# Two layers of graph network on one Trainium2 core: the state's halves are turned by transposing transfers instead of 32x32 blocks and a trip through DRAM

## The chip, the core and the metric

The kernel runs on one core of a Trainium2 chip. Its engines are TensorE (PE, matrix products), VectorE (DVE), ScalarE (ACT), GpSimd (POOL) and SyncE (SP), which here only issues transfers. The metric is the device time of one execution in microseconds (us), as the median of several runs; lower is better.

## The reference

The input x holds 32 independent sequences of 512 nodes with 128 features, and adj is one 512x512 matrix of zeros and ones that all share. Layer 0 is attention over the graph, layer 1 five steps of a gated recurrence. Each starts from a layer norm with a ReLU, and each is added to x:

```
h = relu(layernorm(x));  x = x + leaky(softmax(mask(adj) + leaky(e_src + e_dst)) @ (h W) + b)
h = relu(layernorm(x))
repeat 5 times:
    m  = adj @ h                       # the same for "in" and "out"
    z  = sigmoid([m, m] w3^T + b3 + h u3^T + bu3)
    r  = sigmoid([m, m] w4^T + b4 + h u3^T + bu3)
    hv = tanh([m, m] w5^T + b5 + (r*h) u5^T + bu5)
    h  = (1 - z) h + z hv
x = x + h
```

## The kernel before

The state of a sequence in layer 1 is kept twice. `hT` (128 features on the partitions, 512 nodes along them, float32) feeds the gates and is updated in place. The product with adj needs the other layout, nodes on the partitions, and it needs it as two float16 halves, `hi` (h rounded) and `lo` (what the rounding left), so that eight float16 matmuls with `adjT` give m (L1032). After each step `hT` must therefore be turned and split again before the next step of this sequence can begin.

A step of `recurrence(b, step, ...)` runs so: eight matmuls for m, a copy of it by ScalarE (`mT`, L1043), two products for the r gate (`g`, L1051 and L1052) and its tanh (L1057), r times h by VectorE (`rh`, L1064), the z gate (L1072) and its tanh (L1084), two products for the candidate (`v`, L1095 and L1096) and its tanh (`hv`, L1102), and three VectorE instructions for the new `hT` (L1109, L1115, L1118). Sigmoids are made of tanh, with the weights scaled for it.

`hT` is turned in one of two ways. The direct way is four 128x128 transposes by TensorE into PSUM (`h`, L1156), from where the halves are cast and subtracted. The other way is a VectorE transpose of 32x32 blocks (`blocks`, L1170), one store to DRAM (`way`, L1176), four loads that put the blocks into place (`rows`, L1181), and then the same cast by ScalarE (`hi`, L1009) and subtraction by VectorE (`lo`, L1007). Which way a turn goes is decided by this line, with SHORT = 3 and SHORT_END = 4:

```
nth = 5 * b + WIDTH * step
if nth < 5 * SHORT or (step >= STEPS - 2 and b >= B - SHORT_END):
```

WIDTH is 6, so the direct way is taken for six turns of the first sequences, and for the last two steps of the last four. After the fifth step the turned h goes to the output: for 28 sequences through blocks and DRAM too, then scaled and added to x1.

Layer 0 of a sequence (norm, turn, products hp and av, attention weights) is woven between the steps of others. About six sequences are under way at once, in ten slots of state. Each piece of work is a Task with an engine, an estimated length, a key (its due time), the tasks that it needs and the buffers that it takes. `plan` simulates the engines with the estimates of COST and the landing times (LANDING = 5000 ns for a transfer) and fixes the order of every engine's instructions at build time; on the chip each engine goes through its own list in this order and waits where a needed result is late. SP's list holds the loads of x, the transfers of the turns and the stores of results; POOL's holds the transfers of layer 0's turns.

Of the kernel before, what the change touches and what calls it, by code (L numbers as in the profile page):

```python
# [10 lines left out]
F32 = mybir.dt.float32  # L11
F16 = mybir.dt.float16
AF = mybir.ActivationFunctionType
ALU = mybir.AluOpType

P = 128
# [10 lines left out]
WIDTH = 6  # L27
SLOTS = 10
DIRECT = 4
SHORT = 3  # L30
ENDING = 1
SHORT_END = 4
EARLY = 6
# [13 lines left out]
}  # L47
FIRST_IDLE, IDLE = 32, 36
LANDING = 5000
BRANCH = 150  # L50

WAIT = {"DVE": 200, "ACT": 200}
BANKS = {"m": 2, "g": 3, "v": 2, "o": 4, "bank": 8}
BUFFERS = {
    "x": 4, "h0": 2, "h0T": 2, "hw": 3, "pt0": 2, "pt1": 2, "pt2": 2, "pt3": 2, "o_": 2, "hN": 2,
    "es": 2, "lines": 2, "blocks": 2, "rows": 3, "res": 2, "mT": 4, "r": 2, "rh": 3, "z": 3,
    "hv": 2, "d": 2, "way": 4, "turn": 4, "line": 4,
}


# [224 lines left out]
def gat_then_gated_gnn_kernel(  # L285
# [20 lines left out]
    nc = tc.nc  # L306
    B, N, D = x.shape
# [10 lines left out]
    pools = {  # L318
        n: fast.enter_context(tc.tile_pool(name=f"w{n}", bufs=n)) for n in set(BUFFERS.values())
    }  # L320
    dram = fast.enter_context(tc.tile_pool(name="dram", bufs=4, space=bass.MemoryType.DRAM))
    psum = fast.enter_context(tc.tile_pool(name="psum", bufs=8, space=bass.MemoryType.PSUM))
    pin = tc.keep_in_program_order
    tasks = []

    def add(*args, **kwargs):
        tasks.append(Task(*args, **kwargs))
        return tasks[-1]

    def new(buffer, name, shape=(P, N)):  # L330
        tag = buffer.tags[0]
        if "bank" in buffer.tags:
            buffer.tile = psum.tile([P, N], F32, tag="bank", name=name)
        elif tag in ("way", "turn", "line"):
            buffer.tile = dram.tile(list(shape), F32, tag=tag, name=name)
        else:
            buffer.tile = pools[BUFFERS[tag]].tile(list(shape), F32, tag=tag, name=name)
        return buffer.tile


# [30 lines left out]
    hTs = [state.tile([P, N], F32, name=f"hT_{s}") for s in range(SLOTS)]  # L371

    his = [state.tile([P, K, D], F16, name=f"hi_{s}") for s in range(SLOTS)]
    los = [state.tile([P, K, D], F16, name=f"lo_{s}") for s in range(SLOTS)]
# [15 lines left out]
    def load_x(b, key=None, lands=3000):  # L390
        f = Buffer("x")

        def issue():
            pin(nc.sync.dma_start(out=new(f, f"x_{b}", (P, K, D)), in_=x_r[b]))

        needs = () if key else (bias_loaded,)
        load = add("SP", [1], key or 5 * (b - LEAD) * STEP, issue, needs, (f,), lands=lands)
        return f, load
# [35 lines left out]
    def idle():  # L434
        pin(nc.tensor.transpose((f_idle.tile or new(f_idle, "idle"))[:, :P], ident, ident))  # L435
# [14 lines left out]
    def issue():  # L450
        pin(nc.tensor.matmul(
            new(f_as, "as_ps")[:, : 2 * D], lhsT=ones[0:1, :],
            rhs=avecs.rearrange("o i d -> o (i d)"), start=True, stop=True,
        ))
# [263 lines left out]
    def blockwise(dst, src, which, keys, needs, buffers, by_halves):  # L718
# [11 lines left out]
        def store(g):  # L730
            def issue():
                if way.tile is None:
                    new(way, f"turn_{which}", (K * P, P))
                pin(nc.gpsimd.dma_start(  # L734
                    out=way.tile.rearrange("(e r) (g q) -> g r e q", r=Q, g=G)[g],
                    in_=f.tile[ts(g, Q)].rearrange("r (e q) -> r e q", q=Q),
                ))

            return issue

        stores = []
        for g in range(G):
            stores.append(add("POOL", [1], keys(1), store(g), (t,), (f, way),
                              lands=LANDING))

# [5 lines left out]

        return add("POOL", [1], keys(2), load, stores, (*buffers, way), lands=LANDING + 1500)

# [10 lines left out]
    def layer0(b):  # L764
# [7 lines left out]
        def keys(i):  # L772
            return begin + length * (base[0] + i) / parts
# [77 lines left out]
        else:  # L851
# [11 lines left out]
            def store(k):  # L863
                def issue():
                    if way.tile is None:
                        new(way, f"line_{b}", (K, P))
                    pin(nc.gpsimd.dma_start(
                        out=way.tile[k].rearrange("(g q) -> g q", g=G),
                        in_=f_lines.tile[k * rep :: Q],
                    ))  # L870

                return issue

            stores = []
            for k in range(K):
                stores.append(add("POOL", [1], keys(1), store(k), (t,),
                                  (f_lines, way), lands=LANDING))

# [5 lines left out]

            t = add("POOL", [1], keys(2), spread, stores, (way, f_es), lands=LANDING + 1500)
        base[0] = 15
# [126 lines left out]
    def recurrence(b, step, halved, turned):  # L1013
# [5 lines left out]
        def keys(i):  # L1019
            return key + i * STEP / 4  # L1020

        hT = hTs[b % SLOTS]
# [16 lines left out]
        high, low = halved  # L1039
# [29 lines left out]
        last = step == STEPS - 1  # L1069
# [66 lines left out]
        if near:  # L1136
            t_keep = add("DVE", [512], keys(3.5) - STEP, keep, (t_z,), (f_z, f_d))
            t = add("DVE", [512], keys(5), gated_hv, (t, t_z), (f_z, f_hv))
            turned = add("DVE", [512], keys(5), twice, (t, t_keep), (f_hv, f_d))
            to_turn = f_d  # L1140
        else:
            t = add("DVE", [512], keys(5), differ, (t,), (f_hv, f_d))
            t = add("DVE", [512], keys(5), gated, (t, t_z), (f_z, f_d))
            turned = add("DVE", [512], keys(5), update, (t,), (f_d,))
            to_turn = None

        nth = 5 * b + WIDTH * step
        if nth < 5 * SHORT or (step >= STEPS - 2 and b >= B - SHORT_END):

            f = Buffer("o", "bank")  # L1150

            def turn():
                h_ps = new(f, f"h_{b}_{step}")
                h = to_turn.tile if to_turn else hT
                for k in range(K):
                    pin(nc.tensor.transpose(h_ps[:, ts(k, P)], h[:, ts(k, P)], ident))  # L1156

            needs = (add("PE", [256] * K, keys(6), turn, (turned,),
                         (f, to_turn) if to_turn else (f,)),)
            view = ("p k d -> p k d", {})  # L1160

            def src():
                return f.tile.rearrange("p (k d) -> p k d", k=K)
        else:


            f_b, way, f = Buffer("blocks"), Buffer("way"), Buffer("rows")

            def blocks():
                pin(nc.vector.transpose(  # L1170
                    new(f_b, f"blocks_{b}_{step}").rearrange("p (g k q) -> p g k q", g=G, k=K),
                    hT.rearrange("p (k g q) -> p g k q", g=G, k=K),
                ))

            def store():
                pin(nc.sync.dma_start(out=new(way, f"way_{b}_{step}"), in_=f_b.tile))  # L1176

            def load(g):
                def issue():
                    rows = f.tile or new(f, f"rows_{b}_{step}", (P, G, N // G))  # L1180
                    pin(nc.sync.dma_start(  # L1181
                        out=rows[ts(g, Q)],
                        in_=way.tile.rearrange("(a q) (g e) -> g q a e", a=G, g=G)[g],
                    ))

                return issue

            t = add("DVE", [512], keys(6), blocks, (turned,), (f_b,))
            t = add("SP", [1], keys(6), store, (t,), (f_b, way), lands=LANDING)
            needs = []  # L1190
            for g in range(G):
                needs.append(add("SP", [1], keys(6), load(g), (t,), (way, f),
                                 lands=LANDING))
            view = ("p k (a q) -> p a k q", {"a": G})

            def src():
                return f.tile.rearrange("p a (k q) -> p a k q", k=K)

        if not last:
            return halves(b, src, keys(8), needs, (f,), view[0], **view[1]), turned  # L1200
        f_res = Buffer("res")

        def lower():
            res = new(f_res, f"res_{b}", (P, K, D))
            pin(nc.scalar.mul(res.rearrange(view[0], **view[1]), src(), 1 / LIFT))
# [4 lines left out]
        def result_at_once():  # L1210
            pin(nc.vector.scalar_tensor_tensor(
                new(f_res, f"res_{b}", (P, K, D)), src(), (0.5 if near else 1) / LIFT,
                x1s[b % SLOTS], ALU.mult, ALU.add,
            ))
# [4 lines left out]
        else:  # L1219
            finished[b] = add("DVE", [512], keys(8), result_at_once, needs, (f, f_res))  # L1220
        add("SP", [1], keys(8), lambda: pin(nc.sync.dma_start(out=out_r[b], in_=f_res.tile)),
            (finished[b],), (f_res,), lands=LANDING)

    def ending(b, keys, t_rh, t_z, buffers):

# [82 lines left out]
    for b in range(B):  # L1308
        halved, turned = layer0(b)
        for step in range(STEPS):  # L1310
            made = recurrence(b, step, halved, turned)
            if made:
                halved, turned = made
    order = plan(tasks)
    for t in order[:-BRANCH]:
        t.issue()

    general = nc.values_load(flag[0:1, 0:1])
    for t in order[-BRANCH:]:
        t.issue()  # L1320
# [44 lines left out]
```

## Time and profile before

| | before |
|---|---|
| median of 3 runs | 1141.48 us (1141.41 to 1142.08) |
| span of the profiled execution, first to last instruction | 1139.7 us |
| what the median has beside that span | 1.8 us |
| TensorE busy | 1133.1 us, 99% |
| VectorE busy | 946.9 us, 83% |
| ScalarE busy | 659.3 us, 58% |
| GpSimd busy | 350.7 us, 31% |
| moved by transfers | 132.88 MB, mean 117 GB/s |

The profile is of one execution. Its page gives the busy time of each engine, the busy share in 40 slices of the span, the chain of work that ended last, followed back from the last instruction, and the costliest groups of instructions: line, engine, operation, tiles, shapes and count, then the busy time in us and the mean of one in ns, then the idle time of the engine just before them and what ended it. For transfers it gives the time from issue to landing. Of which of the runs the profile was taken is not told; the 1.8 us are the difference between their median and its span. The timeline lists instructions in order of time. A matmul's record runs on while the next one has begun, so the records overlap.

### The profile page before, as it was taken

To read this page: it belongs to the slowest core of one execution; us is meant where nothing else is said; L and a number is where in the kernel's file an instruction comes from. 1 tells how busy PE (TensorE), PEld (TensorE's weight loads), DVE (VectorE), ACT (ScalarE), POOL (GpSimd) and SP (SyncE) were. 2 spreads that over 40 slices of the span, in tenths; PEclk is the share of its full clock that TensorE was granted. 3 is DMA by queue.
4 is the path that set the end of the run, shared out by engine and by line. 5 is a ranking of instruction groups with operands and counts; after the bars stand their busy time and mean duration, and the time that the engine had idled before them with its cause. 6 is when DMAs were issued, how large, how long until landed. Compare 5 with 4: busy or idle time off the path is not lost.

```text
span 1139.7 us, 15186 instructions
## 1 busy us (share of the span) xinstructions
PE 1133.1 (99%) x4373; PEld 599.0 (53%) x4373; DVE 946.9 (83%) x2124; ACT 659.3 (58%) x1297; POOL 350.7 (31%) x503
## 2 busy tenths in 40 slices
PE   9999999999999999999999999999999999999998
PEld 8665554555455545555554555546555555444444
DVE  7888988889789888987898878989898998765764
ACT  6755566555755665564656645575656655554553
POOL 4345324132424234341443315243455321100000
PEclk9999999999999999999999999999999999999999
DMA  3114435353445444443444435444445433332311
GB/s 107 45 49 118 131 106 145 109 142 114 139 115 151 121 139 130 125 125 111 141 138 138 122 110 146 144 132 129 131 128 154 129 103 103 103 98 76 112 37 66
DMA packets 133915, 132.88 MB, mean 117 GB/s; under 512 B 22082, under 2 KB 97988, under 8 KB 133700
## 3 DMA queue, kind: packets, MB, share of 16 engines
q1 hardware_dynamic: 116066, 94.89, 26.6%
q0 software_dynamic: 17472, 36.79, 13.1%
q8 instruction: 36, 0.59, 0.2%
q14 instruction: 51, 0.42, 0.1%
q10 hardware_dynamic: 290, 0.20, 0.1%
HBM read 70.39 MB, written 61.40 MB: 116 GB/s over the span
## 4 chain that ended last, share of the span: by engine, by line
PE 99%; ACT 0%; DVE 0%; issue 0%; POOL 0%; POOLq 0%; DVEq 0%
PE m L1032 24%; PE g L1072 12%; PE g L1051 12%; PE g L1052 12%; PE v L1096 12%; PE v L1095 12%; PE av L923 10%; PE hp L807 3%; PE idle L435 1%; PE h L1156 0%; PE t_a L702 0%; PE t_b L702 0%; PE v_end L1256 0%; PE es L842 0%; PE end L1274 0%; PE at_ps L489 0%
## 5 line engine op out<-in xcount | busy, mean ns | idle before, releaser
L1057 ACT ACTIVATE rs<-g,zrb 128x512 f32<-128x512 f32 x160 | 109.8, 686 | 142.0 <-PE g L1052 138.7
L1102 ACT ACTIVATE hv<-v,vb 128x512 f32<-128x512 f32 x159 | 109.0, 686 | 124.1 <-PE v L1096 123.8
L1051 PE MATMUL g<-hT,u3T 128*128 128x512 f32 x320 | 163.5, 592 | 0.0
L1052 PE MATMUL g<-mT,w4sT 128*128 128x512 f32 x320 | 163.4, 592 | 0.0
L1072 PE MATMUL g<-mT,w3dT 128*128 128x512 f32 x320 | 163.2, 594 | 0.0
L1032 PE MATMUL m<-adjT,hi 128*128 128x512 f16 x640 | 162.4, 379 | 0.0
L1095 PE MATMUL v<-mT,w5sT 128*128 128x512 f32 x318 | 162.4, 592 | 0.0
L1096 PE MATMUL v<-rh,u5hT 128*128 128x512 f32 x318 | 162.4, 592 | 0.0
L1032 PE MATMUL m<-adjT,lo 128*128 128x512 f16 x640 | 161.5, 379 | 0.0
L1043 ACT COPY mT<-m 128x512 f32<-128x512 f32 x160 | 93.6, 585 | 113.6 <-PE m L1032 112.8
L1064 DVE SCALAR_TENSOR_TENSOR rh<-rs,hT 128x512 f32<-128x512 f32 x160 | 108.5, 682 | 54.3 <-ACT rs L1057 53.8
L1109 DVE SCALAR_TENSOR_TENSOR d<-hv,hT 128x512 f32<-128x512 f32 x158 | 107.5, 681 | 54.4 <-ACT hv L1102 53.9
L1084 ACT ACTIVATE zs<-g,zrb 128x512 f32<-128x512 f32 x160 | 109.7, 685 | 64.0 <-PE g L1072 63.1
L923 PEld LDWEIGHTS av<-hw,pt 128*128 128x128 f32 x1024 | 122.2, 191 | 16.6 <-issue 12.7
L923 PE MATMUL av<-hw,pt 128*128 128x129 f32 x1024 | 123.8, 275 | 0.2 <-ACT adjT L498 0.2
L1118 DVE SCALAR_TENSOR_TENSOR hT<-d,hT 128x512 f32<-128x512 f32 x158 | 109.2, 691 | 11.8 <-PE m L1032 0.5
L1032 PEld LDWEIGHTS <-hi 128*128 128x128 f16 x640 | 62.6, 98 | 102.2 <-issue 49.5
L1115 DVE SCALAR_TENSOR_TENSOR d<-zs,d 128x512 f32<-128x512 f32 x158 | 109.1, 691 | 4.8
L1032 PEld LDWEIGHTS <-lo 128*128 128x128 f16 x640 | 62.7, 98 | 88.1 <-issue 22.7
L645 POOL TENSOR_TENSOR rs_b<-ve_b,mhalf 128x4 f32<-128x4 f32 x32 | 36.2, 1132 | 228.2 <-DVE ve_b L625 195.2
L1170 DVE STREAM_TRANSPOSE blocks<-hT 128x512 f32<-128x512 f32 x146 | 102.8, 706 | 4.1 <-DMA way<-blocks 1.4
L734 POOL DMA_DIRECT2D turn_b<-blocks_b x112 | 73.8, 664 | 91.0 <-DVE blocks_b L724 89.3
(140 smaller groups left out, 1434.0 us busy)
## 6 DMA issues: line engine op xcount, KB each, us to landing
way<-blocks SPq DMA_DIRECT2D x146, 256.0 KB, 2.0
rows<-way SPq DMA_DIRECT2D x584, 64.0 KB, 2.2
x<-in_x_dram SPq DMA_DIRECT2D x32, 256.0 KB, 2.8
out_dram<-res SPq DMA_DIRECT2D x31, 256.0 KB, 2.0
turn_a<-blocks_a POOLq DMA_DIRECT2D x112, 64.0 KB, 2.2
h0T<-turn_a POOLq DMA_DIRECT2D x28, 256.0 KB, 3.6
es<-line POOLq DMA_DIRECT2D x28, 256.0 KB, 4.0
turn_b<-blocks_b POOLq DMA_DIRECT2D x112, 64.0 KB, 2.5
```

The source lines that it names most:

```text
L923: pin(nc.tensor.matmul(avs()[:, i, :], lhsT=f_pts[c].tile[:, ts(2 * part + i, P)], rhs=hw()[:, c, : D + 1], start=start, stop=(c == K - 1) ...
L1032: pin(nc.tensor.matmul(f_m.tile, lhsT=part[:, k, :], rhs=adjT[:, k, :], start=(first and k == 0), stop=(not first and k == K - 1),))
L1051: pin(nc.tensor.matmul(g, lhsT=u3T, rhs=hT, start=True, stop=False))
L1052: pin(nc.tensor.matmul(g, lhsT=w4sT, rhs=f_mT.tile, start=False, stop=True))
L1057: pin(nc.scalar.activation(new(f_r, f"rs_{b}_{step}"), f_g.tile, AF.Tanh, bias=rb, scale=0.5))
L1072: pin(nc.tensor.matmul(f_g.tile, lhsT=w3dT, rhs=f_mT.tile, start=False, stop=True, skip_group_check=True))
L1084: pin(nc.scalar.activation(new(f_z, f"zs_{b}_{step}"), f_g.tile, AF.Tanh, bias=zb, scale=0.5))
L1095: pin(nc.tensor.matmul(v, lhsT=w5sT, rhs=f_mT.tile, start=True, stop=False))
L1096: pin(nc.tensor.matmul(v, lhsT=u5hT, rhs=f_rh.tile, start=False, stop=True))
L1102: pin(nc.scalar.activation(new(f_hv, f"hv_{b}_{step}"), f_v.tile, AF.Tanh, bias=vb))
L1115: pin(nc.vector.scalar_tensor_tensor(d, f_z.tile, 1.0, d, ALU.add, ALU.mult))
L1118: pin(nc.vector.scalar_tensor_tensor(hT, f_d.tile, 0.5, hT, ALU.mult, ALU.add))
```

## The change

Turns that are neither direct nor the last of a sequence take a third way, `crossed`. ScalarE casts `hT` to a float16 tile `hiT` in the layout that it has, VectorE subtracts to get `loT`, and two transposing transfers from SP's queue write the halves straight into the matmuls' tiles `hi` and `lo`. The block transposes, the store and the four loads remain only for the output turns of 28 sequences. SHORT goes from 3 to 1, which leaves one direct turn of the first sequences. The plan is told 3600 ns for the landing of a crossing, and three buffers each are made for `hiT` and `loT`. Since the plan is computed from the tasks, the order of all engines changes with them.

```diff
-SHORT = 3
+SHORT = 1
...
+CROSSING = 3600
...
-    "hv": 2, "d": 2, "way": 4, "turn": 4, "line": 4,
+    "hv": 2, "d": 2, "way": 4, "turn": 4, "line": 4, "hiT": 3, "loT": 3,
...
+        elif not last:
+            return crossed(b, step, keys, turned), turned
...
+    def crossed(b, step, keys, turned):
+        hT = hTs[b % SLOTS]
+        f_hi, f_lo = Buffer("hiT"), Buffer("loT")
+        def high():
+            pin(nc.scalar.copy(new(f_hi, f"hiT_{b}_{step}", dtype=F16), hT))
+        def low():
+            pin(nc.vector.tensor_tensor(
+                new(f_lo, f"loT_{b}_{step}", dtype=F16), hT, f_hi.tile, ALU.subtract
+            ))
+        def cross(dst, f):
+            return lambda: pin(nc.sync.dma_start_transpose(out=dst[b % SLOTS], in_=f.tile))
+        t_hi = add("ACT", [480], keys(6), high, (turned,), (f_hi,))
+        t_lo = add("DVE", [512], keys(6), low, (t_hi,), (f_hi, f_lo))
+        return (
+            add("SP", [1], keys(6), cross(his, f_hi), (t_hi,), (f_hi,), lands=CROSSING),
+            add("SP", [1], keys(6), cross(los, f_lo), (t_lo,), (f_lo,), lands=CROSSING),
+        )
```

More of the change, by code (lines that the diff above doesn't have):

```diff
@@ L328, in add, with new @@
         return tasks[-1]
-    def new(buffer, name, shape=(P, N)):
+    def new(buffer, name, shape=(P, N), dtype=F32):
         tag = buffer.tags[0]
@@ L336, in new @@
         else:
-            buffer.tile = pools[BUFFERS[tag]].tile(list(shape), F32, tag=tag, name=name)
+            buffer.tile = pools[BUFFERS[tag]].tile(list(shape), dtype, tag=tag, name=name)
         return buffer.tile
```

## The prediction

> **What bounds the kernel now.** I read the header and the busy table first, then the slices, the chain, the engine waits, and last the timeline of TensorE.
>
> ```profile
> span 1139.7 us, 15186 instructions
> PE 1133.1 (99%) x4373; PEld 599.0 (53%) x4373; DVE 946.9 (83%) x2124; ACT 659.3 (58%) x1297; POOL 350.7 (31%) x503
> ...
> PE   9999999999999999999999999999999999999998
> ...
> PEclk9999999999999999999999999999999999999999
> ...
> PE 99%; ACT 0%; DVE 0%; issue 0%; POOL 0%; POOLq 0%; DVEq 0%
> ```
>
> TensorE (PE) is busy in every slice at full clock, and the chain that ended last is TensorE for 99%. The waits of TensorE say the same: three in the whole span, 1.8 us together.
>
> ```profile
> PE idle L435 <- POOL ident masks.py:199: 1.4, 1, 1.4
> PE av L923 <- ACT adjT L498: 0.2, 1, 0.2
> PE end L1274 <- DVE gated L1267: 0.2, 1, 0.2
> ```
>
> So only two things move the time: matmuls taken from TensorE, and stalls given to it. What VectorE (DVE), ScalarE (ACT) and the queues gain is worth nothing by itself. The timeline around one turn of h prices a matmul by the start of the next one, since the records overlap (its columns are start, duration, line):
>
> ```profile
> 62.60 1.03 PE L1032 MATMUL m<-adjT,hi 128*128 128x512 f16 x4
> 63.47 0.60 PE L1156 MATMUL h<-ident,hT 128*128 128x128 f32 x4
> 63.90 1.03 PE L1032 MATMUL m<-adjT,lo 128*128 128x512 f16 x4
> 64.77 1.03 PE L1032 MATMUL m<-adjT,hi 128*128 128x512 f16 x4
> ```
>
> The turn lasts 0.60 but costs 63.90 - 63.47 = 0.43 us (0.437 to the nanosecond). In the same way four f16 matmuls of m cost 0.865 and one f32 product with 512 columns (two records) 0.859.
>
> **What the Trainium skill says.** Trainium Kernel Development and Optimization, Performance Expectations, calls matmul busy time a bad metric because matmuls are pipelined. The trace agrees (0.60 recorded, 0.437 paid), so I use starts. DMA: Bandwidth & Descriptors, DMA Transpose (X-bar), says that a transposing transfer takes 2-byte data only: hence the split into f16 halves must come ahead of the turn. No transfer of this kind is in the trace of before.
>
> **The change, part by part.**
>
> 1. Turns taken from TensorE. A turn is made on TensorE where 5b + 6·step < 5·SHORT. With SHORT = 3 that holds for 0, 5, 6, 10, 11 and 12, six turns; with 1 only for 0. Five turns x 0.437 = **-2.19 us**. The trace shows the five at 49.95, 56.02, 63.47, 79.00 and 84.73 us, with no gap beside them, so all of it is on the path.
>
> 2. The plan is computed anew with the other costs, so TensorE's order moves. I measured in the written order of the changed program how much TensorE work lies between a result and its user, priced by the spacings above. Before, the z gate (L1072) follows its r gate so closely in three places that it waits for the tanh: at 549.3, 687.6 and 863.1 us the spacings exceed their medians by 0.04, 0.15 and 0.18 us. In the new order there is 1.1 us or more between them everywhere, save in the last sequence, which is as before. About **-0.37 us**; bounds 0 and -0.4. All other users inside a step keep more than they need (tanh to r·h to candidate needs some 1.85 us).
>
> 3. The turn's route. Removed, for 118 turns: one VectorE block transpose, one store and four loads.
>
> ```profile
> L1170 DVE STREAM_TRANSPOSE blocks<-hT 128x512 f32<-128x512 f32 x146 | 102.8, 706 | 4.1 <-DMA way<-blocks 1.4
> ...
> way<-blocks SPq DMA_DIRECT2D x146, 256.0 KB, 2.0
> rows<-way SPq DMA_DIRECT2D x584, 64.0 KB, 2.2
> ```
>
> VectorE loses 118 x 0.706 = 83 us. Casts and subtractions stay 160 each, with hT as their source (612 and 681 ns now). All this is cover, not path: 0. The queue of SyncE (SP) loses 118 stores at 0.34 us and 472 loads at 0.44 to 0.46 us of issue (about 250 us together) and gets 246 transposing transfers; POOL's queue issues as many transfers as before. Queued behind a crossing on SP are only other crossings, loads of x and stores of results.
>
> 4. The new wait. The first matmul of m for the next step waits for a crossing, and TensorE works in order, so a late crossing stops everything. From the end of the candidate's product: 0.2 us until its tanh starts, 3.0 until hT is written (median of before, 2.84 to 5.8), 0.61 for the cast of the high half, some 0.1 for two hand-overs: **3.9 us + T**, T being issue to landing. The low half needs 0.7 more, and its matmuls come at least 0.86 later. What the new order leaves between the two, tightest first (sequence, step):
>
> - (31,0): 8.60 us, ten f32 products; (31,1): 8.61
> - (30,0): 9.53; (1,0): 9.96; (3,0): 11.6; (0,1): 11.8
> - then 15.5 and more; the median is 28.
>
> Before, the tightest crossing through DRAM had 17.2, and the trace shows its cast ending 0.3 us ahead of its matmul; the new order allows half that way. With the ScalarE work that stands ahead of the casts, (31,0) and (31,1) hold until T = 4.6, (30,0) until 5.3, (1,0) until 5.6, the rest beyond 7.5.
>
> T is not in the trace. Lower end: a plain store of blocks lands in 2.0. Upper end: the Trainium skill, VectorE: DVE Perf Modes, The three transpose paths, prices one 128x128 bf16 square at 1309 ns; a half is four squares, so 5.2 if nothing overlaps. DMA: Bandwidth & Descriptors, Latency and other measured facts, gives 261 GB/s for transposing transfers, 0.5 us for 128 KB. I take 2.0 + 1.3 = 3.3 us, an estimate: one landing and one square that isn't hidden. Stall at 3.3: **0**. At 5.2: 2 x 0.6 = 1.2 us. At 6: 2.8 + 0.7 + 0.4 = 3.9. At 7: 4.8 + 1.7 + 1.4 = 7.9.
>
> 5. Rate. In the steady part, a sequence passes in 34.5 us and crosses four times: eight transfers, one in 4.3 us. At 1.3 to 3.3 us each, the stream has room even if they run strictly one by one.
>
> 6. Traffic. Off DRAM go 118 x 512 KB, 60 of the 132.9 MB; the crossings bring 32 MB between SBUF tiles. The other transfers can only land sooner, which TensorE never waited for: 0. Should crossings slow a neighbour on the 16 engines, its cover is the same 15 us and more.
>
> 7. The head (TensorE waits for data with filler transposes until 30 us, same order) and the tail (from about 1087 us the same order) stay.
>
> Sum on the profiled span: 1139.7 - 2.19 - 0.37 = 1137.1 us. The median of the three runs lies 1.8 us above that span (1141.48), so I expect 1141.48 - 2.56 = **1138.9 us**.
>
> **The rivals.**
>
> A. No stall, as above: 1138.5 to 1139.3 (the second if part 2 gives nothing). 0.2% is 2.28 us, about what a measurement of this kernel can tell from no change, so this case falls on both sides of it: with part 2 faster, without it no change. For it: every slack but four is above 11 us. Chance 0.65, of which 0.45 faster.
>
> B. Crossings a little late, T from 4.6 to 6: stalls at four places take back the gain or a little more, 1138.9 to 1142.8. For it: four squares in a row are 5.2 us. Chance 0.12, within 0.2% for 0.10.
>
> C. The slower side: **landing late at the last sequences and the first**. Place: m of (31,1), (31,2), (30,1) and (1,1), which have no other sequence's work to hide behind. Price: 4(T - 5.03) from T = 5.6 on (the sum of the four shortfalls), so it outweighs the gain of 2.56 from T = 5.7 and gives 1142.8 at 6 us, 1146.8 at 7 and more beyond, where (3,0) and (0,1) join. Against it: the plain store's 2.0 us and the 261 GB/s. For it: hi and lo of one turn, sometimes of two turns, go one behind another ((28,1) directly before (30,0)), so the last may wait for the first. Chance 0.15.
>
> D. The stream becomes the bound: above 4.2 us of occupation each (1030 us between first and last crossing over 246) it alone sets the time. At the 5.2 of unhidden squares 246 x 5.2 = 1279 us, plus 45 at the head and 75 at the tail: 1400 us. Chance 0.08.
>
> **How the numbers follow.** Faster by over 0.2%: A's 0.45. Within: 0.20 of A and 0.10 of B, 0.30. Slower: 0.02 of B, C and D, 0.25. The range runs from 1138.2 (A with all of part 2 and what small waits of the head may give) to 1147.0 (C at T = 7); D, C beyond 7 us and a larger gain are left out, some 0.17.
>
> **What would show it.** Right: 32 transposes of h in place of 52, the block transposes at 28, crossings landing in 3 to 4 us, no TensorE wait on a transfer, busy TensorE some 2.5 us less. Wrong: in the waits of TensorE, m L1033 waiting for a DMA, near 45 to 60 us (case C, first sequences) or past 960 us (last); all over the span, with SP's issue row at 4 us or more, case D. A z gate that still waits at mid-span would undo part 2.

## The result, and the profile after

| | before | after |
|---|---|---|
| median of 20 runs each | 1141.55 us | 1139.35 us |
| lowest and highest | 1140.93 to 1144.15 | 1138.7 to 1141.69 |
| profiled execution, its span | 1139.7 us | 1139.9 us (that execution took 1141.68) |
| landing of a transposing transfer | none | 2.5 us |

Ratio after / before: 0.9981, 95% interval 0.9975 to 0.9987. The change gains 2.2 us (0.19%), and the interval is clear of 1; a gain of 2.56 us, to 1138.9, was forecast.

The two profiled spans don't show that gain: after's is the longer one. I read header, slices and chain first, as before:

```profile
span 1139.9 us, 14320 instructions
PE 1133.1 (99%) x4353; PEld 600.4 (53%) x4353; DVE 873.0 (77%) x2006; ACT 662.3 (58%) x1297; POOL 347.4 (30%) x503
...
PE   9999999999999999999999999999999999999998
...
PE 99%; ACT 0%; issue 0%; DVE 0%; POOL 0%; POOLq 0%; DVEq 0%; ACTq 0%
```

TensorE has 20 matmuls less (4373 to 4353: five turns of four) and the same busy time to the digit. Matmuls taken away and nothing gained would need a stall, but the waits of TensorE after are the three of before, and none of them is for a transfer:

```profile
PE idle L436 <- POOL ident masks.py:199: 1.4, 1, 1.4
PE av L924 <- ACT adjT L499: 0.2, 1, 0.2
PE end L1300 <- DVE gated L1293: 0.2, 1, 0.2
```

So the same matmuls must have run slower somewhere. The timeline of TensorE over the first 12 us shows where (start, duration, engine, line). Before:

```profile
1.37 3.96 PE L435 MATMUL idle<-ident 128*128 128x128 f32 x18 [1.37 <-POOL ident masks.py:199]
5.25 0.69 PE L451 MATMUL as_ps<-avecs,ones 1*128 1x256 f32 x2
5.88 1.31 PE L435 MATMUL idle<-ident 128*128 128x128 f32 x10
```

The same view of after:

```profile
1.36 4.10 PE L436 MATMUL idle<-ident 128*128 128x128 f32 x18 [1.36 <-POOL ident masks.py:199]
5.39 1.22 PE L452 MATMUL as_ps<-avecs,ones 1*128 1x256 f32 x2
6.54 2.40 PE L436 MATMUL idle<-ident 128*128 128x128 f32 x10
...
10.44 0.80 PE L490 MATMUL at_ps<-ident,a_sb 128*128 128x128 f32 x4
```

The ten filler transposes take 1.31 us before and 2.40 us after: TensorE reaches its full rate at about 5.3 us in one execution and at about 10.9 us in the other. Nothing of the change lies that early. The Trainium skill, TensorE: Matmul & The Clock Gate, in the section on the clock gate, says that a cold TensorE runs at half rate until a window of about 3.4 us has been busy. The half rate is what both traces show: a filler takes 0.22 us from start to start at first, and 0.11 later. But the date at which it ends differs by 5.6 us between two executions whose TensorE is busy from 1.4 us on, and the later one has half rate for 9.5 us, nearly three times the page's window.

It is chance, not the change: the runs of *both* kernels fall into two groups. Of before's 20, 15 lie at 1140.9 to 1142.1 (median 1141.41) and five at 1143.35 to 1144.15; of after's 20, 14 at 1138.7 to 1139.9 (median 1139.10) and six at 1141.1 to 1141.7. The profiled execution of after is of the upper group; that of before, by its span and the usual 1.8 us beside it, of the lower one. Eight traces can be placed so, and all agree: full rate begins at 5.05 to 5.25 us in the four of lower groups (before, experiments 4, 5 and 11), at 10.2 to 11.6 us in the four of upper groups (after, experiments 1, 2 and 3). What makes it early or late is not shown. Group against group the change gains 2.31 us in the lower and 2.14 in the upper one.

The trace can still be used: measure from a point past the head. From the start of the first z gate, of (0,0), to the start of the last products into `end`, just ahead of the end:

| kernel | first z gate | last products into `end` | stretch |
|---|---|---|---|
| before | 30.31 | 1133.65 | 1103.34 |
| after | 32.88 | 1133.65 | 1100.77 |

The stretch is 2.57 us shorter; the prediction's sum was 2.56. That the two agree to 0.01 us is luck: each stretch is of one execution, and the terms as measured (part 2 below) make 2.49. The experiments below are read by this stretch too.

The new transfers, from the part of after's page on transfers (columns: KB each where given, us to landing) and from the view of the issuing line (duration in ns min/median/max, first and last start):

```profile
way<-blocks SPq DMA_DIRECT2D x28, 256.0 KB, 2.0
...
hi<-hiT SPq DMA_TRANSPOSE x123, 2.4
lo<-loT SPq DMA_TRANSPOSE x123, 2.6
```

```profile
L1241 SPq DMA_TRANSPOSE hi<-hiT x123: 1188/1196/2207, 52.6 to 1070.7; - x123
L1241 SPq DMA_TRANSPOSE lo<-loT x123: 1188/1207/2019, 54.0 to 1072.9; - x123
...
DMA to landing us min/median/max: 2.4/2.5/6.9
```

A half lands in 2.5 us, half a microsecond more than a plain store, but SP is held 1.2 us by each issue, against 0.34 for a plain store.

### The profile page after: what moved, and what is told of

Read it like the earlier page. It is cut to its first block, busy times and chain, and to the rows that moved or that the text cites. A ratio compares the mean times of both kernels' runs of the same rounds, so it can differ in the third digit from the quotient of the medians.

```text
span 1139.9 us, 14320 instructions
## 1 busy us (share of the span) xinstructions
PE 1133.1 (99%) x4353; PEld 600.4 (53%) x4353; DVE 873.0 (77%) x2006; ACT 662.3 (58%) x1297; POOL 347.4 (30%) x503
## 2 busy tenths in 40 slices
DMA packets 182774, 103.21 MB, mean 91 GB/s; under 512 B 146466, under 2 KB 161956, under 8 KB 182564
## 3 DMA queue, kind: packets, MB, share of 16 engines
q1 hardware_dynamic: 164930, 65.26, 23.6%
## 4 chain that ended last, share of the span: by engine, by line
PE 99%; ACT 0%; issue 0%; DVE 0%; POOL 0%; POOLq 0%; DVEq 0%; ACTq 0%
PE m L1033 24%; PE g L1073 12%; PE g L1052 12%; PE g L1053 12%; PE v L1096 12%; PE v L1097 12%; PE av L924 10%; PE hp L808 3%; PE idle L436 1%; PE h L1157 0%; PE t_a L703 0%; PE t_b L703 0%; PE v_end L1282 0%; PE at_ps L490 0%; PE es L843 0%; PE end L1300 0%
## 5 line engine op out<-in xcount | busy, mean ns | idle before, releaser
L1073 PE MATMUL g<-mT,w3dT 128*128 128x512 f32 x320 | 163.6, 593 | 0.0
L1053 PEld LDWEIGHTS g<-mT,w4sT 128*128 128x128 f32 x320 | 60.8, 190 | 76.5 <-issue 70.5
L1097 PEld LDWEIGHTS v<-rh,u5hT 128*128 128x128 f32 x318 | 60.4, 190 | 76.1 <-issue 66.5
```

Of the source, the lines that this page charges most:

```text
L1053: pin(nc.tensor.matmul(g, lhsT=w4sT, rhs=f_mT.tile, start=False, stop=True))
L1073: pin(nc.tensor.matmul(f_g.tile, lhsT=w3dT, rhs=f_mT.tile, start=False, stop=True, skip_group_check=True))
L1097: pin(nc.tensor.matmul(v, lhsT=u5hT, rhs=f_rh.tile, start=False, stop=True))
```

## The experiments

Eleven kernels ran. Each was compared with the kernel before on the same chip, and every ratio is to that. "Excess" is the sum, between 30 and 1080 us of the trace, of what the spacings of TensorE's matmuls (start to next start) exceed the median of their kind, the same line, tiles and shape: before 0.32 us, after 0.02.

### 1 and 2. Each half of the change alone

The route alone, edit of after:

```diff
-SHORT = 1
+SHORT = 3
```

> The crossings stay, but SHORT goes back to 3, so TensorE makes six of the first sequences' turns again. My theory (the gain is matmul work taken from TensorE, the route is worth nothing by itself): TensorE has the 2.19 us again, the z gates are spaced well in this order too (no distance under 0.97 us before the last sequence), so 0.0 to 0.4 us faster than the kernel before, some 2.2 slower than the changed one: 1141.1 to 1141.5. Rival (the route itself brings the time, through less VectorE work and 30 MB less traffic): stays with the changed kernel, about 1139.3.

Measured: 1144.08 us, ratio 1.0018 (1.0011 to 1.0024). It is 2 us *slower* than before, which neither of the two expectations had. Its waits of TensorE:

```profile
PE h L1157 <- DVE kept L1133: 1.7, 1, 1.7
PE idle L436 <- POOL ident masks.py:199: 1.4, 1, 1.4
PE g L1073 <- ACT rs L1058: 0.7, 1, 0.7
PE av L924 <- DVE pt L893: 0.6, 1, 0.6
```

The one at L436 is that of every kernel's start. The other three are new, and none is for a crossing: a z gate (L1073) at 831.9 us that follows its r gate too closely, an `av` at 868.4, and the last turn, which stands still from 1137.7 us for VectorE. The planner got the new landing times, with the five turns still to be made on TensorE, and the order that it found has its own gaps. They make 3.0 us; the stretch from the first z gate to the end of the span grows by 2.1 (from 1109.4 to 1111.5), and the 0.9 between is not taken apart.

SHORT alone, edit of before:

```diff
-SHORT = 3
+SHORT = 1
```

> The kernel before with SHORT = 1 and nothing else: five turns less on TensorE, but the way through blocks and DRAM. My theory (the faster route is what lets the turns go): the same 2.19 us leave TensorE, but in the written order z gate (1,1) stands directly behind its r gate, that of (1,2) 0.45 us and that of (2,1) 0.86 us behind it, so about 1.4 us of waiting for the tanh come in near 62, 86 and 93 us, and the m of (1,1), (0,2) may wait for loads; in all 0.8 us faster to 2 us slower than before. Rival (the turns could have gone without the new route): 2.2 us faster than before, 1139.3, no new gap on TensorE.

Measured: 1145.88 us, ratio 1.0024 (1.0014 to 1.0033). Slower again, though the same five turns are gone. Its waits of TensorE:

```profile
PE g L1072 <- ACT rs L1057: 1.8, 3, 0.8
...
PE av L923 <- DVE pt L892: 0.7, 1, 0.7
PE m L1032 <- DVE lo L1007: 0.4, 1, 0.4
PE m L1032 <- ACT hi L1009: 0.3, 1, 0.3
```

The excess is 5.08 us, with z gates at 68.6, 95.1 and 103.1 us for 2.33 of it. -2.19 for the turns, +5.08 and -0.32 for the excess make +2.6; the same stretch grows by 2.60 (from 1109.4 to 1112.0).

So the gain is not a sum of halves: +2.0 us (medians) and +2.6 (stretch) alone, -2.2 together. The rival that the turns could simply have been dropped without the new route falls, for the order that this planner finds.

### 3. The five turns put back

The plan and the order of after, with the 20 transposes of the five turns issued again on TensorE, into the bank of `m` ahead of the matmuls that overwrite it. Edit of after:

```diff
+ if step and 0 < 5 * b + WIDTH * (step - 1) < 15:
+     for k in range(K):
+         pin(nc.tensor.transpose(f_m.tile[:, ts(k, P)], hT[:, ts(k, P)], ident))
```

> The changed kernel in its own order, with the twenty transposes of the five dropped turns put back: each group of four runs on TensorE directly ahead of the m that uses the turned state, into m's bank, which the first matmul then overwrites (their result is not used). My theory (the gain is these matmuls' time, and everything else in the order is cover): 5 x 0.437 = 2.19 us slower than the changed kernel, so 1141.5, about the kernel before. Rival (the gain came from the new order's spacing, and early TensorE time is partly waiting): 0.0 to 1.2 us slower than the changed kernel, since the transposes would fill the gap that the plan fills with transposes near 90 us.

Measured: 1142.16 us, ratio 0.9999 (0.9991 to 1.0008). The gain is gone. The stretch is 1136.71 - 33.52 = 1103.19, so the 20 transposes cost 2.42 us, where 5 x 0.437 is 2.19. The 0.23 between is in the spacings: the excess is 0.28 us here, most of it at a z gate at 196 us. The gain of the change is TensorE's work on the path; of what else the new route and its order brought, no more than 0.15 us is left (before's stretch is 1103.34).

### 4. Four more turns crossed

After turns the last two steps of the last sequences on TensorE; here the last but one crosses too. Edit of after:

```diff
- if nth < 5 * SHORT or (step >= STEPS - 2 and b >= B - SHORT_END):
+ if nth < 5 * SHORT or (last and b >= B - SHORT_END):
```

> The changed kernel, with the fourth step of the last four sequences crossed too instead of turned by TensorE (four turns less). My theory: 4 x 0.437 = 1.75 us faster than the changed kernel, 1137.6, since the slacks of these crossings in the new order are 15.5 us and more against some 7.6 needed (landing 2.5 us). Rival (the last sequences have nothing to hide behind): TensorE waits for a crossing near 1090 us, no gain or a loss of 1 to 2 us.

Measured: 1137.97 us, ratio 0.9966 (0.9953 to 0.9979). The stretch is 1129.36 - 30.29 = 1099.07, 1.70 us less than after; four turns x 0.437 = 1.75. No new wait came.

### 5. Late fillers taken out

TensorE still runs filler transposes near 90 us; eleven are dropped. Edit of after:

```diff
-FIRST_IDLE, IDLE = 32, 36
+FIRST_IDLE, IDLE = 32, 25
```

> The changed kernel with 57 filler transposes instead of 68: the eleven that the plan put near 90 us, where it foresaw a gap, are left out; the other orders stay. If the gap that the plan foresaw is not there on the chip (the traces show no wait on TensorE): 11 x 0.109 = 1.2 us faster than the changed kernel, 1138.1. If the gap is real: no change, and a wait of TensorE of about 1.2 us near 90 us.

Measured: 1139.59 us, ratio 0.9978 (0.997 to 0.9987): no gain beyond after. The stretch is 1131.25 - 30.57 = 1100.68, 0.1 less. The waits of TensorE show what came in place of 1.2 us of fillers:

```profile
PE av L924 <- DVE pt L893: 0.2, 1, 0.2
PE m L1033 <- DVE lo L1008: 0.2, 1, 0.2
```

The excess is 1.08 us, which takes back nearly all of the 1.2: `m` at 94.2 and 95.3 us (0.53) and `av` at 808.6 us (0.35). In this order the fillers were cover, and 11 of them cost next to nothing.

### 6 to 8. One, two and three spare crossings ahead of each

To find where the stream starts to matter, each crossing is preceded by n transfers of the same half into spare tiles. Edit of after, for n = 1:

```diff
+spare = [state.tile([P, K, D], F16, name=f"spare_{s}") for s in range(8)]
...
- return lambda: pin(nc.sync.dma_start_transpose(out=dst[b % SLOTS], in_=f.tile))
+ def issue():
+     for _ in range(1):
+         pin(nc.sync.dma_start_transpose(out=spare[next(turn_of) % 8], in_=f.tile))
+     pin(nc.sync.dma_start_transpose(out=dst[b % SLOTS], in_=f.tile))
```

> The changed kernel, where every crossing is preceded on SP's queue by one more transfer of the same half into a spare tile; the orders of the other engines stay. From the changed kernel's trace: an issue holds the queue for 1.2 us, the tightest landings are ahead of their matmuls by 1.57 (lo of (31,0)), 1.88 (lo of (31,1)), 1.99 (hi of (30,0)) and 2.33 us. High halves land 1.2 later, low halves 2.4. My theory (the slack in the written order prices the lateness): waits of 0.8 and 0.5 us at the two low halves and up to 1.6 at (30,0), 1.3 to 3 us slower than the changed kernel: 1140.7 to 1142.4. Rival (the queue overlaps transfers and the issue is all that grows): no wait of TensorE on a transfer, 1139.4.

> The same with two more transfers ahead of every crossing: high halves 2.4 later, low halves 4.8. My theory: waits of 3.2 and 2.9 us at (31,0) and (31,1), about 2 at (0,1), 0.4 to 5 at (30,0); 9 to 13 us slower than the changed kernel, 1148 to 1152, and more if the queue is full already, since six issues of 1.2 us are 7.2 of the 8.6 us between two turns. Rival (landing is hidden by more than the order shows): under 4 us slower.

> The same with three more transfers. My theory (SP's issue of 1.2 us per transfer is a rate): 984 issues are 1181 us, with 85 us of other issues 1266, where some 1025 us lie between the first and the last crossing; so the queue becomes the bound and the time is about 240 us longer, 1380. Rival (the issue is a latency that overlaps, the engines' packets count): 1155 to 1200, with TensorE waiting at the tight places alone.

Measured: n = 1: 1172.76 us, ratio 1.0254 (1.0231 to 1.0278). n = 2: 1347.7 us, 1.1817 (1.1787 to 1.1847). n = 3: 1652.1 us, 1.4466 (1.4437 to 1.4494). All three expectations failed: the first was 1.3 to 3 us beyond after and it became 33; the second ended at 1152, the third at 1380. From n = 2 to 3 the time grows by 304 us for 246 transfers, 1.24 us each, and SP's issues by 308 us (1054 to 1362): nearly all of the added issue time is paid. Yet SP is not busy throughout even then. Between the first and the last crossing it issues for 84% of the time with n = 2 and for 87% with n = 3, and in the rest it waits for other engines, as they wait for it. So no run reached the bound of a stream that alone sets the time.

What happened at n = 1? The waits of TensorE first (us in total, times, longest):

```profile
PE g L1075 <- ACT rs L1060: 7.4, 4, 4.3
PE g L1055 <- ACT mT L1046: 5.3, 5, 2.1
PE g L1054 <- DMA hT<-turn_b: 4.8, 3, 3.4
PE av L926 <- DVE pt L895: 3.8, 2, 3.0
PE m L1035 <- DMA lo<-loT: 3.1, 3, 1.5
...
PE m L1035 <- DMA hi<-hiT: 0.8, 1, 0.8
```

Only 3.9 us of these are for crossings; 4.8 are for a turn of layer 0 that comes by POOL's queue (`hT<-turn_b`). The longest, 4.3 us, is for `rs` of ScalarE. One follows it back through three engines. ScalarE's timeline, ahead of that `rs` at 300.63 us:

```profile
298.87 0.62 ACT L1235 CAST hiT<-hT 128x512 f16<-128x512 f32 x1 [4.67 <-DVE hT L1121]
...
300.63 0.69 ACT L1060 ACTIVATE rs<-g,zrb 128x512 f32<-128x512 f32 x1
```

It stood 4.67 us for VectorE's `hT`. VectorE's timeline:

```profile
295.85 0.87 DVE L619 BATCH_NORM_STATS2 st_a<-x 128x6 f32<-128x128 f32 x4 [4.28 <-DMA x<-in_x_dram]
296.64 0.67 DVE L1112 SCALAR_TENSOR_TENSOR d<-hv,hT 128x512 f32<-128x512 f32 x1
...
298.14 0.69 DVE L1121 SCALAR_TENSOR_TENSOR hT<-d,hT 128x512 f32<-128x512 f32 x1
```

VectorE stood 4.28 us for a load of x, the input of a later sequence, with the `d` and `hT` of running sequences behind it. And SP's timeline shows where that load was issued:

```profile
285.43 1.19 SPq L1245 DMA_TRANSPOSE spare<-hiT  x1
286.71 1.27 SPq L1246 DMA_TRANSPOSE hi<-hiT  x1
288.07 1.22 SPq L1245 DMA_TRANSPOSE spare<-loT  x1
289.38 1.22 SPq L1246 DMA_TRANSPOSE lo<-loT  x1
290.70 0.53 SPq L1186 DMA_DIRECT2D rows<-way  x1
291.32 0.38 SPq L397 DMA_DIRECT2D x<-in_x_dram  x1
```

It stood in line behind four transposing transfers, two of them spares, and landed some 4.5 us after its issue (median of such loads here 2.9, after 2.7). Over the whole span VectorE's waits for loads of x are, in this kernel and then in after:

```profile
DVE st_a L619 <- DMA x<-in_x_dram: 29.8, 8, 4.9
```

```profile
DVE st_a L617 <- DMA x<-in_x_dram: 5.5, 5, 2.6
```

### 9. The spare crossing behind the real one

Same transfers as in 6, but the spare follows, so no crossing is put back by its own spare:

```diff
  def issue():
+     pin(nc.sync.dma_start_transpose(out=dst[b % SLOTS], in_=f.tile))
      for _ in range(1):
          pin(nc.sync.dma_start_transpose(out=spare[next(turn_of) % 8], in_=f.tile))
-     pin(nc.sync.dma_start_transpose(out=dst[b % SLOTS], in_=f.tile))
```

> As with one more transfer per crossing, but the spare one is issued behind the real one, so that high halves land as in the changed kernel and low halves 1.2 us later, which the tightest margin of 1.57 still covers. In the trace with the spare one ahead, TensorE waited for crossings for 3.9 us only; VectorE waited 29.8 us for loads of x, which stand behind crossings on SP's queue. My theory now (the extra transfers hurt through what is queued behind them and through the shared engines, not through late crossings): still most of the 33 us, 1155 to 1172. Rival (the crossings' own lateness was the cause): 1139 to 1141.

Measured: 1167.28 us, ratio 1.0234 (1.0209 to 1.0258). Most of the 33 us stays, and so does VectorE's wait for x, 29.9 us. That a crossing is late by its own spare is not the main cause.

### 10. Loads of x on another queue

The kernel of 6, with the loads of x of the sequences from 7 on issued by POOL. Edit of that kernel:

```diff
- pin(nc.sync.dma_start(out=new(f, f"x_{b}", (P, K, D)), in_=x_r[b]))
+ queue = nc.sync if b < 7 else nc.gpsimd
+ pin(queue.dma_start(out=new(f, f"x_{b}", (P, K, D)), in_=x_r[b]))
```

> One more transfer ahead of every crossing as before, but the loads of x from sequence 7 on are issued from POOL's queue, at the same place of the plan. If the loads of x behind the crossings on SP's queue make the loss (VectorE stands still for them in its own order, then ScalarE's casts and tanh are late, then TensorE): 1141 to 1155, and VectorE's waits for x shrink to the 5 us of the changed kernel. Rival (all transfers are slowed by the share of the engines, 42% for this queue in place of 24%; POOL's turns of layer 0 landed at 5.3 in place of 3.5 us): 1160 to 1175.

Measured: 1147.19 us, ratio 1.0048 (1.0033 to 1.0063); 25.6 of the 33 us beyond after have gone. The Trainium skill, DMA: Bandwidth & Descriptors, in the section on issuing engines, says that these are not separate DMA engines and that spreading transfers over them saves issue time only. This case agrees, and shows what issue time can be worth: the shared engines are loaded as before (SP's queue took 41.5% of them in 6, 40.6% here; after: 23.6%), so it is not their load that went.

Did the loads lose their time in SP's line of issues, or behind the crossings' packets once issued? The move took them out of both, but the traces of 6 and after tell. In 6, seven loads of x besides the very first make VectorE wait, 27.1 us together. Each stands at the end of an unbroken line of SP's issues, and is issued 3.0 to 5.6 us after the VectorE addition that frees its buffer (L980); in after the four such loads are issued 0.7 to 2.0 us after it. From the issue on they take 3.0 to 4.5 us until VectorE starts on them, against 2.9 to 3.1 in after. So the line of issues is the larger part, and a later landing the smaller. The waits now, of VectorE:

```profile
DVE st_a L620 <- DMA x<-in_x_dram: 8.6, 7, 2.6
```

and of TensorE:

```profile
PE m L1036 <- DMA lo<-loT: 3.2, 3, 1.7
PE g L1076 <- ACT rs L1061: 1.3, 2, 1.1
PE m L1036 <- DMA hi<-hiT: 0.7, 1, 0.7
```

What is left for crossings is 3.9 us. These waits are at the places that the slack table gives, (30,0), (31,0) and (31,1), and a little longer than the 1.3 to 3 us expected from it in 6. TensorE's wait for layer 0's turns is gone, though these still land late (`h0T` in 5.0 us, 3.5 in after), so it did not come from their landing alone. The stretch of this execution, the fastest of the four at 1145.09 us, is 1137.52 - 30.32 = 1107.20, 6.4 more than after; the spacings put 4.6 of that on the crossings and 1.9 on two z gates.

### 11. The three together

No direct turn at the start, the end crossed, fillers out. Edit of after:

```diff
-SHORT = 1
+SHORT = 0
...
-FIRST_IDLE, IDLE = 32, 36
+FIRST_IDLE, IDLE = 32, 25
...
- if nth < 5 * SHORT or (step >= STEPS - 2 and b >= B - SHORT_END):
+ if nth < 5 * SHORT or (last and b >= B - SHORT_END):
```

> The changed kernel with no direct turn at the start (SHORT = 0), the fourth step of the last four sequences crossed, and 57 fillers in place of 68: five turns less than the changed kernel, 5 x 0.437 = 2.19 us. The first crossing, (0,0), has 8.3 us in the new order, against 6.4 needed (3.9 and a landing of 2.5). My theory: 2.2 us faster than the changed kernel, 1137.1, within 1 us for waits that the newly planned order brings or drops. Rival (early and late crossings have nothing to hide behind, and the order brings its own waits as with the route alone): 1139 or more, with waits of TensorE before 60 or past 960 us.

Measured: **1136.27 us**, ratio 0.9952 (0.9938 to 0.9965), the fastest kernel of this study: some 3 us below after. The stretch is 1127.53 - 30.11 = 1097.42, 3.35 us less than after. Five turns x 0.437 and 11 fillers x 0.109 make 3.38. The expectation, 1137.1, had counted the turns alone. The fillers, worth nothing in experiment 5, are worth their whole price here, since this order brings no wait for them to cover (excess 0.06 us). Its waits of TensorE are again the three of before:

```profile
PE idle L436 <- POOL ident masks.py:199: 1.4, 1, 1.4
PE av L924 <- ACT adjT L499: 0.2, 1, 0.2
PE end L1300 <- DVE gated L1293: 0.2, 1, 0.2
```

The tightest crossing whose landing is recorded, the low half for (30,0), lands 0.56 us ahead of its matmul: little is left to take on this way.

## Why the prediction was right, point by point

**Turns (part 1): right.** 20 matmuls gone, and putting them back takes the gain away (experiment 3). The price from starts (0.437 us) held three times: 2.19 against 2.42 measured, 1.75 against 1.70, and within 0.03 us of the sum in experiment 11. The recorded busy time would have given 5 x 0.60 = 3.0 us. The sign named for it, a busy TensorE some 2.5 us less, did not show (1133.1 in both), since the half rate lasted longer in after's profiled execution.

**Plan (part 2): right.** The z gates' waits are gone: the excess falls from 0.32 to 0.02 us, so 0.30 in place of 0.37. The stretch fell by 2.57 in all, 0.08 more than 2.19 and 0.30. Experiments 1 and 2 show how little this could be taken for granted: two neighbouring orders of the same planner carry about 3 and 5 us of waits. It was known ahead only because the written order of after was measured.

**Route (part 3): right in its result, off in its terms.** VectorE's busy time fell by 73.9 us (946.9 to 873.0), not 83. The block transposes did take 83 us with them, but busy time counts overlapping records once, and neighbours overlapped by 106 us before and by 100 after; the other instructions took 3 us more. Its worth was zero, as forecast. On SP, the issue of a transposing transfer was not priced. It is 1.2 us, so that SP issues for 394 us in after, 330 before. The sentence that only other crossings, loads of x and stores stand behind a crossing was correct, but no price was put to the loads of x.

**Wait (part 4): right, with the term T mis-sized.** T was 2.5 us, not 3.3; 2.5 lies in the bounds of 2.0 and 5.2. The places were right: landing to first matmul, read from the trace, the tightest are the low halves for (31,0), 1.57 us, and (31,1), 1.88, then the high half for (30,0), 1.99. (61 of the 246 landings are not recorded; the low half for (30,0) is among them, and by its issue and the usual 2.4 to 2.6 us it has 1.4 to 1.6.) The table gave (31,0) 4.6 - 2.5 = 2.1 at this T. The half microsecond between is SP's issue time, which the table left out: the low half for (31,0) is issued 1.32 us behind its high half, and its matmuls come only 0.87 us later. Rivals B and C needed T above 4.6 and 5.6 and didn't happen.

**Rate (part 5) and rival D: the verdict right, the margin wrong.** One transfer in 4.3 us is carried without a trace of it. But the threshold of D, an occupation of 4.2 us with 1400 us as its price, was not where the kernel breaks: two transfers of 1.2 us in the place of one already cost 33 us (experiment 6). The step that failed is the cover: the slack table lists only what TensorE has ahead of it, and is right for that in the places and nearly in the size (3.9 us in experiment 10). What breaks first is the load of x in SP's line, and then VectorE and ScalarE, which work in order.

**Traffic, head and tail (parts 6 and 7): right but for one thing.** Traffic fell from 132.9 to 103.21 MB, worth nothing (118 x 512 KB is 61.9 MB, where the prediction has 60). The head was called unchanged, and its order is; but the date of TensorE's full rate moves the whole time by 2.3 to 2.4 us between executions of one kernel (medians of the two groups), as much as the gain. The sum was set against a median of three runs of before that all were of the lower group (1141.41 to 1142.08); one of the upper group as the base would have put the forecast 2 us off. That the base was of the group of most runs is in part luck.

**The chances.** A with part 2, a gain of more than 0.2%, had the highest chance. The medians give 0.19%, just on the other side of that mark, and 1139.35 lies 0.05 us above A's own range. The stretch and the waits show A with part 2 all the same; with runs in groups 2.3 us apart, the medians cannot decide on which side of such a mark the gain lies.

## What to carry to other kernels

In a kernel like this one, with one engine busy to 99%, a change is worth the work that it takes from that engine, priced by spacings and not by recorded durations, plus or minus the waits of the new order; so compute the new order before believing either half of a change, and try the halves together. When a transfer is put on an in-order queue, ask not only who waits for it but what stands behind it in that queue, and which in-order engine will stand still for that one. When spans differ by a few microseconds, compare a stretch that begins after TensorE has reached its full rate.

## What the runs showed of the hardware

- A transposing transfer of 128x512 float16 between SBUF tiles lands in 2.4 to 2.6 us (medians of after) and holds the issuing SP for 1.2 us; 246 more of them cost this kernel 1.24 us each (experiment 8 against 7). Four squares of 128x128 do not cost four times a square's 1309 ns, which the Trainium skill (VectorE: DVE Perf Modes, The three transpose paths) gives.
- TensorE's full rate began at about 5.3 us in one profiled execution and at about 10.9 us in another, with TensorE busy from 1.4 us on in both; the other traces lie near one or the other (5.05 to 5.26, 9.6 to 11.6). The row of the granted clock is 9 in all 40 slices for both, so only the durations of the first matmuls show it.
- The kernels in which TensorE waits most have a lower granted clock too: mean 0.999 in after, 0.949 with two spare crossings and 0.871 with three. The same 4353 matmuls were busy for 1133.1, 1188.6 and 1243.9 us.
